# Layer 3 of a graph network as one stream: aligned node tiles summed in PSUM, PSUM operands for VectorE, nodes finished in the edge loop, experts by groups

## The chip, the core and the metric

The kernel runs on one core of a Trainium2 chip. Its engines are TensorE (PE), VectorE (DVE), ScalarE (ACT), GpSimd (POOL) and SyncE (SP); each works through its own queue of instructions in order, and semaphores make one wait for another. Layer 3's ordinary loads and stores are issued by SP, the indirect gathers and the accumulating writes by POOL. The metric is the device time of the whole program in microseconds (us); lower is better.

## The reference

Four layers, each a graph layer and a feed-forward layer, work on 3125 nodes of 256 float32 features. The graph has 50,000 edges, and one loop per node is added. The change is to layer 3, which is a graph attention (one row per edge, eight heads of 32) with a batch norm over the nodes, and then a mixture of four experts beside a shared network:

```python
e = jax.nn.leaky_relu(a_src[src] + a_dst[dst], NEG_SLOPE)
m = jax.ops.segment_max(e, dst, num_segments=N)
e = jnp.exp(e - m[dst])
denom = jax.ops.segment_sum(e, dst, num_segments=N)
alpha = e / denom[dst]
msg = xh[src] * alpha[:, :, None]
out = jax.ops.segment_sum(msg, dst, num_segments=N).reshape(N, H * D) + bias
out = (out - mean) * jax.lax.rsqrt(var + BN_EPS) * gamma + beta
...
gates = jax.nn.softmax(x @ gW + gb, axis=-1)
topv, topi = jax.lax.top_k(gates, TOPK)
topw = jax.nn.softmax(topv, axis=-1)
return shared + gated
```

The graph layer's input is the layer norm of x, and its result is added to x; the experts' input is again a layer norm of x, and their output is added to x too.

## The kernel before

Nodes lie in NT = 25 tiles of P = 128 rows. Edges are sorted by destination in an earlier layer and, with the loops, make ET = 416 tiles of 128, so that a tile's destinations lie close together. EL = 8 edge tiles are a chunk; there are NW = 52 chunks. Layers 0 to 2 come first and are nearly untouched. The end of layer 2 writes, for each node, a row of 264 numbers (projected features and a source term for each head) to DRAM as `xa_d`, and the destination terms, split into three bf16 parts, to `a_d` (`next_project`, lines 1003 to 1017). In layer 0's feed-forward part a table `acc3_d` of sums is filled with zeros (lines 1127 to 1130).

**The edge loop** is in `l3_gnn_sorted` (L547). The order of the work is that of the Python loop `for c in range(NW + LAG)` with LAG = 4: each engine takes its instructions in the order in which this loop makes them, and buffers of the pools (`bufs=`) set the waits. In iteration c:

- For chunk c, POOL gathers eight tiles of source rows from `xa_d` into the buffer `xa` (helper `gather`, L194), which has LAG + 3 = 7 copies. SP loads the destination numbers `dl`, from which DVE makes a bf16 one-hot `sT` (L384), and 128 rows of destination terms `aw` (L575): a window W0[c] that holds all destinations of the chunk. PE multiplies the two (`pa`, L582). DVE reduces the three parts (L585), adds the source terms once the gathers have landed (L589), and takes leaky ReLU and the maximum with the loop's own term (L590, L591: `top`).
- Every second iteration, `segment_max` takes two chunks at once: three transposes on PE (L405), two scans on DVE (L409, L410) and a maximum (L413). In the other iterations `segment_back` transposes it back, DVE subtracts (L604), ACT takes the exponential into the last columns of `xa` (L607), and DVE masks the loop's own term (L609).
- For chunk b = c - LAG, DVE multiplies features by exponentials in place (L616, 128 x 2048 elements, both operands in SBUF), makes a float32 one-hot of the destinations within the window (`onehot`, L390, comparing `iota` and `dloc`, both in SBUF), PE sums the edges of the window by eight products into `acc` (helper `mm`, L141), ACT copies it (L426), and POOL writes it to `acc3_d` by a DMA that adds (L427, `accumulate`). A window is not aligned with the node tiles, so a node's sum may be spread over several windows.

**After the loop**, DVE reads the sums back five tiles at a time (`fin`, L627), divides (L631 to L642), PE transposes each node tile (L646) and DVE takes its statistics (L647); `l3_norm` makes scale and shift, spreads them over the partitions, and DVE applies them and adds x tile by tile (L661 to L665). `l3_ffn` (L1784) then works through all nodes stage by stage: layer norm and transposes (L182, L189), logits (L1806), softmax (from L1702), the two largest of four (`first_max`), weights and their transposes (L1817 to L1828). Only then does it go by GROUPS of four node tiles (the seventh has one): shared layers and experts (L1836, L1852), the spread weights `pk` (L1857), the product `he` (L1859), the output product `po` and the addition to x (L1868), and the store.

Of the kernel before, what the change touches and what calls it, by code (L numbers as in the profile page):

```python
# [8 lines left out]
F32 = mybir.dt.float32  # L9
BF = mybir.dt.bfloat16  # L10
# [7 lines left out]
P = 128  # L18
# [8 lines left out]
EL = 8  # L27
# [8 lines left out]
W0 = [min(max(round(N * (g + 0.5) * EL * P / E) - P // 2, 0), NP - P) for g in range(NW)]  # L36

# [4 lines left out]
class Net:  # L42


    def __init__(self, ctx, tc, ins, out):
# [51 lines left out]
        self.acc3_d = self.dram.tile([NP, D + 16], F32, name="acc3_d")  # L97
# [216 lines left out]
    def prepare_flags(self):  # L314
# [4 lines left out]
        with ExitStack() as ctx:  # L319
# [28 lines left out]
            sums = work.tile([P, 3], F32, name="sums")  # L348
# [3 lines left out]
            out = work.tile([P, 2, ET], F32, name="out")  # L352
            nc.vector.tensor_scalar(out[:, 0], self.dloc, 0.0, None, op0=ALU.is_lt)
            nc.vector.tensor_scalar(out[:, 1], self.dloc, float(P - 1), None, op0=ALU.is_gt)
            nc.vector.tensor_reduce(sums[:, 1:3], out, axis=AX.X, op=ALU.add)
            nc.vector.tensor_reduce(sums[:, 0:1], sums, axis=AX.X, op=ALU.add)
# [38 lines left out]
    def segment_max(self, load, work, psum, al, s):  # L395
# [7 lines left out]
        aT = psum.tile([P, 3, P], F32, name="aT", bufs=1)  # L403
# [143 lines left out]
    def l3_gnn_sorted(self, wp):  # L547
        nc, tc = self.nc, self.tc
        bias = self.spread(wp, "L3_gnn_bias")
        gamma = self.plain(wp, "L3_gnn_gamma")  # L550
        beta = self.plain(wp, "L3_gnn_beta")
        R = D + 8
        with ExitStack() as ctx:
            xa_d, a_d, acc_d = self.xa_d, self.a_d, self.acc3_d
            big = ctx.enter_context(tc.tile_pool(name="big", bufs=1))
            xh = big.tile([P, NT, D], F32, name="xh")
            nc.sync.dma_start(xh, xa_d[:, :D].rearrange("(t p) d -> p t d", p=P))
            with ExitStack() as ctx1:
                big1 = ctx1.enter_context(tc.tile_pool(name="big1", bufs=1))
                load = ctx1.enter_context(tc.tile_pool(name="load", bufs=2))  # L560
                work = ctx1.enter_context(tc.tile_pool(name="work", bufs=3))
                psum = ctx1.enter_context(tc.tile_pool(name="psum", bufs=2, space=PSUM))

                top = big1.tile([P, ET + 2, 8], F32, name="top")
                nc.vector.memset(top[:, 0:1, :], -BIG)
                nc.vector.memset(top[:, ET + 1:, :], -BIG)
                LAG = 4
                xas, als = {}, {}
                mm = None
                for c in range(NW + LAG):  # L570
                    if c < NW:
                        t = c * EL
                        sT = self.window(load, c)
                        aw = load.tile([P, 48], BF, name="aw")
                        nc.sync.dma_start(aw, a_d[W0[c]:W0[c] + P, :, :]  # L575
                                          .rearrange("p i k -> p (i k)"))
                        xa = work.tile([P, EL, R + 8], F32, name="xa", bufs=LAG + 3)
                        xas[c] = xa
                        pa = psum.tile([P, EL, 3, 16], F32, name="pa")
                        for j in range(EL):  # L580
                            self.gather(xa[:, j, :R], xa_d, self.idx["src"][:, t + j:t + j + 1])
                            nc.tensor.matmul(pa[:, j].rearrange("p i k -> p (i k)"),  # L582
                                             sT[:, j * P:(j + 1) * P], aw, start=True, stop=True)
                        ao = work.tile([P, EL, 16], F32, name="ao", bufs=LAG + 1)
                        nc.vector.tensor_reduce(ao, pa.rearrange("p t i k -> p t k i"), axis=AX.X,  # L585
                                                op=ALU.add)
                        als[c] = ao
                        a = ao[:, :, :8]
# [1373 lines left out]
```

## Time and profile before

| what | value |
|---|---|
| runs, median of 3 | 4257.59 us (4254.7 to 4267.4) |
| the profiled execution: its own time | 4221.33 us |
| its span, first to last instruction | 4219.4 us |
| mean granted TensorE clock | 0.884 |
| busy: PE, DVE, ACT, POOL | 3351.4, 2125.7, 928.4, 1830.7 us |
| layer 3, first gather starts | 3171.94 us |
| last gather starts; DVE takes it up (L589) | 3846.98; 3851.34 us |
| last `acc` copied; last tile's statistics end | 3877.64; 3921.23 us |
| first scale and shift (L661) | 3925.1 us |
| expert groups begin to end in steps of | 30.5 us |

The page comes from one execution. A group names line, engine, operation, output and inputs, count, busy time, mean ns of one, and the idle time before it with what ended it. The slices cut the span into 40 parts of 105.5 us; a digit is the busy share in tenths, and PEclk is the clock that TensorE was granted, in tenths of full. The chunks repeat in pairs, because the segment maximum takes two.

### The profile page before, as it was taken

How to read it: one execution, taken by the hardware profiler on the slowest of the kernel's cores; microseconds unless marked ns; L12 is line 12 of the kernel's file. 1: busy time of each engine (PE TensorE's matmuls, PEld its weight loads, DVE VectorE, ACT ScalarE, POOL GpSimd, SP SyncE). 2: the span in 40 equal slices, each digit the busy share in tenths (PEclk: the TensorE clock that was granted, in tenths of full speed). 3: DMA queues.
4: the chain of work that ended last, by engine and by line, in shares of the span. 5: the costliest groups of instructions: out<-in, count | busy, mean ns of one | idle time of the engine just before them, and what ended most of it. 6: DMA issues, size and time to landing. Idle time of an engine off the chain costs nothing. (4 is left out here: it accounts for less than half of the span.)

```text
span 4219.4 us, 45504 instructions
## 1 busy us (share of the span) xinstructions
PE 3351.4 (79%) x15090; PEld 2224.8 (53%) x15090; DVE 2125.7 (50%) x5044; ACT 928.4 (22%) x1995; POOL 1830.7 (43%) x1561
## 2 busy tenths in 40 slices
PE   3598899999982649999999989999993434345599
PEld 2364377777761526666666645665562223223344
DVE  4672499999994354333333332233233444446610
ACT  2222200000001224333333323333330000000122
POOL 4200166666652037777777730000007888884000
PEclk7799999999996859999999999999995676777589
DMA  4641488888861867777777750000005555554000
GB/s 127 208 142 51 159 286 279 271 282 270 277 194 53 245 186 148 122 122 121 122 121 122 118 128 2 6 6 6 6 12 163 121 121 123 122 123 98 15 15 17
DMA packets 364151, 539.24 MB, mean 128 GB/s; under 512 B 75453, under 2 KB 271107, under 8 KB 363907
## 3 DMA queue, kind: packets, MB, share of 16 engines
q0 software_dynamic: 132528, 244.16, 27.8%
q1 hardware_dynamic: 223987, 284.74, 21.4%
q10 hardware_dynamic: 7392, 7.34, 0.5%
q8 instruction: 123, 2.02, 0.2%
q14 instruction: 121, 0.99, 0.1%
HBM read 393.40 MB, written 142.67 MB: 127 GB/s over the span
## 5 line engine op out<-in xcount | busy, mean ns | idle before, releaser
L194 POOL DMA_INDIRECT xa<-xa_d,src_i x416 | 504.1, 1212 | 819.7 <-DMA dl<-dlT_d 693.6
L794 POOL DMA_INDIRECT t<-sm,to x416 | 662.4, 1592 | 259.6 <-ACT sm L791 171.2
L194 POOL DMA_INDIRECT kv<-kv_d,src_i x416 | 418.4, 1006 | 604.0 <-DVE s L390 348.9
L141 PE MATMUL pf<-L_gnn_Wf,hf 128*128 128x256 f32 x1664 | 451.8, 394 | 0.0
L141 PE MATMUL pe<-L_gnn_We,ea 128*128 128x256 f32 x1664 | 437.5, 385 | 12.4 <-DMA ea<-in_edge_attr_dram 9.7
L780 DVE TENSOR_TENSOR xs<-xs,pf 128x512 f32<-128x512 f32 x208 | 142.8, 687 | 430.6 <-PE pf L141 429.0
L141 PEld LDWEIGHTS pe<-L_gnn_We,ea 128*128 128x128 f32 x1664 | 291.4, 192 | 67.2 <-DVE kv L504 26.9
L141 PEld LDWEIGHTS pf<-L_gnn_Wf,hf 128*128 128x128 f32 x1664 | 284.3, 191 | 50.0 <-ACT hf L742 0.5
L141 PEld LDWEIGHTS <-sT 128*128 128x128 bf16 x2496 | 240.4, 98 | 113.9 <-issue 22.8
L405 PE MATMUL aT<-ident,top 128*128 128x128 f32 x78 | 25.7, 395 | 339.3 <-DVE top L591 339.2
L141 PE MATMUL acc<-xa,s 128*128 128x272 f32 x832 | 258.3, 466 | 30.0 <-ACT acc_o L426 16.1
L504 DVE TENSOR_TENSOR kv<-kv,pe 128x1024 f32<-128x1024 f32 x208 | 250.2, 1203 | 4.9 <-PE pe L141 4.9
L426 ACT COPY acc_o<-acc 128x264 f32<-128x264 f32 (+1 forms) x104 | 39.7, 382 | 916.3 <-PE acc L141 485.7
L789 PE MATMUL ps<-xs,m 128*128 128x256 f32 x832 | 235.2, 405 | 1.6 <-DVE xs L780 0.8
L791 ACT COPY sm<-ps 128x512 f32<-128x512 f32 x208 | 121.7, 585 | 509.8 <-PE ps L789 428.7
L531 PE MATMUL acc<-kv,s 128*128 128x264 f32 x832 | 225.0, 395 | 11.1 <-DVE kv L526 8.9
L952 ACT ACTIVATE h<-ph,L_ffn_b,bn_r 128x512 f32<-128x512 f32 (+1 forms) x224 | 162.6, 731 | 290.7 <-PE ph L141 290.2
L141 PEld LDWEIGHTS acc<-xa,s 128*128 128x128 f32 x832 | 183.5, 231 | 79.3 <-ACT acc_o L426 24.6
L980 DVE SCALAR_TENSOR_TENSOR xres<-po,v,xres 128x256 f32<-128x256 f32 x200 | 96.1, 482 | 248.0 <-PE po L141 247.8
L589 DVE TENSOR_TENSOR ao<-ao,xa 128x64 f32<-128x64 f32 x52 | 11.7, 225 | 398.0 <-DMA xa<-xa_d,src_i 395.0
L405 PEld LDWEIGHTS aT<-ident,top 128*128 128x128 f32 x78 | 13.1, 181 | 357.8 <-DVE top L591 349.9
L141 PE MATMUL po<-L_ffn_Wo,h 128*128 128x256 f32 x800 | 196.2, 389 | 0.0
(400 smaller groups left out, 5868.7 us busy)
## 6 DMA issues: line engine op xcount, KB each, us to landing
ea<-in_edge_attr_dram SPq DMA_DIRECT2D x52, 1024.0 KB
dl<-dlT_d SPq DMA_DIRECT2D x156, 256.0 KB
row<-src_d SPq DMA_DIRECT2D x52, 512.0 KB
xs_d<-zero SPq DMA_DIRECT2D x2, 7168.0 KB
xg<-xs_d SPq DMA_DIRECT2D x28, 512.0 KB
t<-zero SPq DMA_DIRECT2D x4, 3328.0 KB
seg<-seg_d SPq DMA_DIRECT2D x52, 256.0 KB
qw<-q_d SPq DMA_DIRECT2D x52, 192.0 KB
```

The costliest lines, as they stand in the source:

```text
L141: self.nc.tensor.matmul(out, l, r, start=(i == 0), stop=(i == len(pairs) - 1))
L194: self.nc.gpsimd.indirect_dma_start(out=out, out_offset=None, in_=table, in_offset=bass.IndirectOffsetOnAxis(ap=ids, axis=0))
L405: nc.tensor.transpose(aT[:, i, :], al[:, 16 * s + i:16 * s + i + 16, :] .rearrange("p t h -> p (t h)"), self.ident)
L426: nc.scalar.copy(o, acc)
L504: nc.vector.tensor_add(kvv, kvv, pe[:, :, None, :].to_broadcast([P, 2, 2, D]))
L531: nc.tensor.matmul(acc, s1[:, j, :], kv[:, j, D:], start=((t + j) % EL == 0), stop=((t + j) % EL == EL - 1))
L780: nc.vector.tensor_mul(xs, xs, pf)
L789: nc.tensor.matmul(ps[:, j, :], m[:, (2 * c + j) % EL, :], xs[:, j, :], start=True, stop=True)
L791: nc.scalar.copy(sm, ps)
L794: nc.gpsimd.indirect_dma_start(out=tables[(2 * c + j) % len(tables)], in_=sm[:, j, :], in_offset=None, compute_op=ALU.add, out_offset=bass ...
L952: nc.scalar.activation(h[:, f, :w], ph[:, :w], AF.Relu, scale=ab[i][0][:, c:c + 1], bias=ab[i][1][:, c:c + 1])
L980: nc.vector.scalar_tensor_tensor(xv[:, i, :], po[:, i, :], v[:, j + i, e - 2:e - 1], xv[:, i, :], op0=ALU.mult, op1=ALU.add)
```

## The change

`l3_sorted` takes the place of `l3_gnn_sorted`, and `l3_dense` that of `l3_ffn` on this path.

- **Aligned tiles.** A table ENDS says which one or two node tiles an edge tile can touch (SPREAD = 38 nodes to either side of where it would lie if edges were spread evenly; layer 0 gets two more checks that the data keep to it, else the other, unsorted path runs). Each edge tile is multiplied once for each node tile that it can touch: 656 products of a one-hot and `xa` instead of 416, and as many `pa` products. W is the largest number of one-hots in a chunk, 16. A node tile's sum stays in PSUM (`acc`, bufs=3) from its first to its last edge tile: there is no `acc3_d`, no copy, no accumulating DMA and no reload. The bf16 destination terms stay in SBUF (`a3`).
- **PSUM operands.** `iota` is copied once to PSUM, and the exponential is written a second time, to the PSUM tile `back`; the multiply and the one-hots read those.
- **Buffers.** `xa` has LAG + 2 = 6 copies.
- **Nodes in the loop.** When a node tile's last edge tile is summed, the next iteration divides it (`finish`), and the one after transposes it and, every fourth tile, takes statistics (`stats`). Its own rows come by one load per tile.
- **Weights.** The feed-forward weights are loaded in iteration 4 (`l3_weights`); the biases `gb` and `sb3` are split in three bf16 parts (`bias3`), and their products are bf16.
- **Groups.** `l3_dense` does everything by groups of four node tiles: scale, shift and layer norm (`front`), transposes and logits (`turn`), softmax and choice (`choose`), weights' transposes (`spread`), and `experts`. The steps of the next group and the group after stand at three points (hooks) within the experts of a group.

The core of the diff (the loop's unchanged lines are left out, and the checks of layer 0 and the move of the code of layer 2 into a method of its own):

```diff
+PACE = N * P / E
+SPREAD = 38.0
+ENDS = [range(int(max(PACE * (t + 0.5) - SPREAD - 0.1, 0)) // P,
+              int(min(PACE * (t + 0.5) + SPREAD + 0.1, NP - 1)) // P + 1) for t in range(ET)]
-        self.acc3_d = self.dram.tile([NP, D + 16], F32, name="acc3_d")
...
-                        nc.sync.dma_start(aw, a_d[W0[c]:W0[c] + P, :, :]
-                                          .rearrange("p i k -> p (i k)"))
-                        xa = work.tile([P, EL, R + 8], F32, name="xa", bufs=LAG + 3)
...
-                        v = xa[:, :, :D].rearrange("p t (h c) -> p t h c", h=8)
-                        nc.vector.tensor_mul(v, v, xa[:, :, D:R].unsqueeze(3)
-                                             .to_broadcast([P, EL, 8, 32]))
-                        s1 = self.onehot(work, b * EL, EL)
-                        acc = psum.tile([P, R + 8], F32, name="acc")
-                        self.mm(acc, [(s1[:, j, :], xa[:, j, :]) for j in range(EL)])
-                        self.accumulate(work, acc_d, acc, b)
...
+            turn = psum.tile([P, 4, P], F32, name="turn")
+            iota = turn[:, 3, :]
+            nc.vector.tensor_copy(iota, self.iota)
...
+            def finish(T):
+                nonlocal oT
+                acc = accs.pop(T)
+                w = work.tile([P, 2, 8], F32, name="fw")
+                nc.vector.tensor_copy(w.rearrange("p i h -> p (i h)"), acc[:, D:D + 16])
+                den, z = w[:, 0, :], w[:, 1, :]
+                f = work.tile([P, 8], F32, name="fz")
+                nc.vector.tensor_add(den, den, z)
+                nc.vector.tensor_scalar(f, den, 0.0, None, op0=ALU.is_equal)
+                nc.vector.tensor_tensor(w, w, f[:, None, :].to_broadcast([P, 2, 8]), op=ALU.add)
+                nc.vector.reciprocal(den, den)
+                nc.vector.tensor_mul(z, z, den)
+                o = work.tile([P, 8, 32], F32, name="fo", bufs=2)
+                nc.vector.tensor_tensor(o, acc[:, :D].rearrange("p (h c) -> p h c", h=8),
+                                        den.unsqueeze(2).to_broadcast([P, 8, 32]), op=ALU.mult)
+                x4 = xh[:, T, :].rearrange("p (h c) -> p h c", h=8)
+                nc.vector.tensor_tensor(x4, x4, z.unsqueeze(2).to_broadcast([P, 8, 32]),
+                                        op=ALU.mult)
+                nc.vector.tensor_add(x4, x4, o)
+            def stats(T):
+                nonlocal oT
+                g, j = T // 4, T % 4
+                if j == 0:
+                    oT = work.tile([P, 2, 4 * P], F32, name="oT", bufs=1)
+                tp = psum.tile([P, 2, P], F32, name="tp")
+                for f in range(2):
+                    nc.tensor.transpose(tp[:, f, :], xh[:, T, f * P:(f + 1) * P], self.ident)
+                for f in range(2):
+                    nc.scalar.activation(oT[:, f, j * P:(j + 1) * P], tp[:, f, :], AF.Identity,
+                                         bias=bias[:, f:f + 1])
+                if j == 3 or T == NT - 1:
+                    w = min((T + 1) * P, N) - 4 * g * P
+                    for f in range(2):
+                        nc.vector.bn_stats(st[:, f, g, :], oT[:, f, :w])
+            for c in range(NW + LAG + 2):
+                for T in ready2:
+                    stats(T)
+                ready2 = []
+                for T in ready:
+                    finish(T)
+                    ready2.append(T)
+                ready = []
+                if c == 4:
+                    self.l3w = self.l3_weights(wp)
...
+                    xa = work.tile([P, EL, R + 8], F32, name="xa", bufs=LAG + 2)
...
+                    sT = load.tile([P, W, P], BF, name="sT")
+                    for T, js, k in parts[c]:
+                        nc.vector.tensor_scalar(sT[:, k:k + len(js), :], row[:, js[0]:js[-1] + 1, :],
+                                                float(W0[c] - T * P), self.part, op0=ALU.add,
+                                                op1=ALU.is_equal)
+                    for T, js, _ in parts[c]:
+                        if T not in seen:
+                            seen.add(T)
+                            nc.sync.dma_start(xh[:, T, :], self.xa_d[T * P:(T + 1) * P, :D])
+                    pa = psum.tile([P, EL, 3, 16], F32, name="pa")
+                    for j in range(EL):
+                        self.mm(pa[:, j].rearrange("p i k -> p (i k)"),
+                                [(sT[:, k + j - js[0], :], self.a3[:, T, :])
+                                 for T, js, k in parts[c] if j in js])
...
+                    back = psum.tile([P, 2, EL, 8], F32, name="back", bufs=2)
+                    nc.tensor.transpose(back.rearrange("p i t h -> p (i t h)"), mm, self.ident)
...
+                        nc.scalar.activation(m, aov[:, :, 0, :], AF.Exp)
...
+                b = c - LAG
+                if 0 <= b < NW:
+                    xa, ex = xas.pop(b), backs.pop(b)
+                    v = xa[:, :, :D].rearrange("p t (h c) -> p t h c", h=8)
+                    nc.vector.tensor_mul(v, v, ex.unsqueeze(3).to_broadcast([P, EL, 8, 32]))
+                    s1 = work.tile([P, W, P], F32, name="s", bufs=2)
+                    for T, js, k in parts[b]:
+                        n = len(js)
+                        t = b * EL + js[0]
+                        nc.vector.scalar_tensor_tensor(
+                            s1[:, k:k + n, :], iota[:, None, :].to_broadcast([P, n, P]),
+                            float(T * P),
+                            self.idxf["dst"][:, t:t + n].unsqueeze(2).to_broadcast([P, n, P]),
+                            op0=ALU.add, op1=ALU.is_equal)
+                    for T, js, k in parts[b]:
+                        begins = T not in accs
+                        if begins:
+                            accs[T] = psum.tile([P, 4 * P], F32, name="acc", bufs=3)
+                        for i, j in enumerate(js):
+                            nc.tensor.matmul(accs[T][:, :R + 8], s1[:, k + i, :], xa[:, j, :],
+                                             start=begins and i == 0,
+                                             stop=last[T] == b and j == js[-1])
+                        if last[T] == b:
+                            ready.append(T)
...
+            def front(g):
+                t0, n = GROUPS[g]
+                xv, ov = self.x[:, t0:t0 + n, :], o[:, t0:t0 + n, :]
+                nc.vector.tensor_mul(ov, ov, ab[:, None, 0, :].to_broadcast([P, n, D]))
+                nc.vector.tensor_add(xv, xv, ab[:, None, 1, :].to_broadcast([P, n, D]))
+                nc.vector.tensor_add(xv, xv, ov)
+                y = work.tile([P, 4, D], F32, name="y")
+                self.normalised(work, y, t0, n)
+                ys[g] = y
+            def turn(g):
+                t0, n = GROUPS[g]
+                y = ys.pop(g)
+                xT = xTs[g] = work.tile([P, 2, 4 * P], F32, name="xT")
+                for j in range(n):
+                    self.transposed(psum, xT, y[:, j, :], j)
+                pl = psum.tile([P, 4, NE], F32, name="sm", bufs=1)
+                for j in range(n):
+                    self.mm(pl[:, j, :], [(xT[:, k, j * P:(j + 1) * P], w_["gW"][:, k, :])
+                                          for k in range(2)] + [(self.ones3, w_["gb"])])
+                ws[g] = pl
...
+                hooks.get(0, lambda: None)()
...
+                    self.mm(po, [(hs[:, c], w_["sW3"][:, 0, :]), (self.ones3, w_["sb3"]),
+                                 (wT[:, j, :], w_["eb3"])]
+                            + [(he[:, i, c], w_["eW3"][:, i, :]) for i in range(2)])
+                    nc.vector.tensor_add(y[:, j, :], self.x[:, t, :], po)
...
+            front(0)
+            turn(0)
+            choose(0)
+            spread(0)
+            front(1)
+            for g in range(NG):
+                hooks = {}
+                if g + 1 < NG:
+                    def early(g=g):
+                        turn(g + 1)
+                        choose(g + 1)
+                    hooks[0] = early
+                    hooks[2] = lambda g=g: spread(g + 1)
+                if g + 2 < NG:
+                    hooks[1] = lambda g=g: front(g + 2)
+                experts(g, hooks)
```

## Prediction

> **What bounds the kernel now.** I read the slices of the span, the groups and the waits first, then the timeline of one steady pair of layer 3's edge chunks, then the tail by windows. The edge loop runs from 3172 to 3851 us (slices 31 to 37 of 40), where POOL leads; behind it come 368 us without POOL, in whose first half the tensor clock is low.
>
> ```profile
> span 4219.4 us, 45504 instructions
> POOL 4200166666652037777777730000007888884000
> PEclk7799999999996859999999999999995676777589
> L194 POOL DMA_INDIRECT xa<-xa_d,src_i x416 | 504.1, 1212 | 819.7 <-DMA dl<-dlT_d 693.6
> ```
>
> The 416 gathers take 1212 ns in the mean, but 948 in the median, so some are delayed. The waits between 3170 and 3880 us show that POOL never stands for a buffer (0.3 us of issue before each gather is all), and that DVE waits for what POOL brings:
>
> ```profile
> POOL xa L194 <- issue: 122.2, 402, 0.3
> DVE ao L589 <- DMA xa<-xa_d,src_i: 395.0, 51, 13.5
> ```
>
> From the timeline of the pair between 3502.69 and 3529.55 us (26.86 us; columns start, us, engine, line):
>
> ```profile
> 3506.83 1.95 POOL L194 DMA_INDIRECT xa<-xa_d,src_i  x1 [0.30 <-DVE seg_m L410]
> ...
> 3510.66 2.28 DVE L616 TENSOR_TENSOR xa<-xa 128x2048 f32<-128x2048 f32 x1
> 3510.89 2.86 POOL L194 DMA_INDIRECT xa<-xa_d,src_i  x1 [0.30 <-issue]
> ...
> 3514.06 0.94 POOL L194 DMA_INDIRECT xa<-xa_d,src_i  x1 [0.30 <-issue]
> ...
> 3517.49 1.03 POOL L427 DMA_DIRECT2D acc_d<-acc_o  x1
> ```
>
> The gather at 3510.89 ends 0.81 us after the message multiply L616 (3512.94); one that meets no such DVE operation takes 0.94. A pair is 16 gathers x 1.248 (0.948 + 0.30) = 20.0, two accumulates of 1.0, and 4.9 of delays: 26.9. The loop is POOL's. Layer 1 has the counter-example in its timeline: L504, with one operand in PSUM, runs from 1005.11 to 1006.31, and the gather at 1004.98 beside it takes 0.96.
>
> The tail's windows (PE, weight loads, DVE, ACT, POOL, clock, DMA share, GB/s): DVE alone, then PE at a low clock, then PE at full clock.
>
> ```profile
> 3925.00:3956.00 31.00, 0.72 (x4) 0.67 (x4) 30.88 (x105) 0.66 (x3) 1.17 (x4) 0.50 0.08 23
> 3956.00:4060.00 104.00, 101.61 (x319) 61.21 (x318) 23.05 (x102) 30.39 (x98) 0.00 (x0) 0.66 0.04 10
> 4060.00:4219.00 159.00, 152.29 (x436) 67.05 (x435) 17.12 (x35) 29.41 (x47) 0.00 (x0) 0.99 0.06 20
> ```
>
> [...] L504 with PSUM and L390 without both take 1.20 for 1024 elements[...] at 3503.64 the acc products come 8 in 3.84 us (0.48 each), at 3862 64 in 15.24 (0.238).
>
> **Edge loop, part by part.** From POOL's queue go the two accumulates, 2.0 us a pair. With the iota and a copy of exp in PSUM, multiply and one-hots no longer have two SBUF inputs: of the 4.9 I keep 0.3, for the small operations. These alone would leave 20.3 to 20.8 a pair. But a wait comes in. The xa buffers go from LAG+3 = 7 to LAG+2 = 6, so chunk c's first gather waits for the last acc product of chunk c-6. Those products (call them M) are issued in iteration c-2, where their one-hots stand in DVE's queue behind the add that waits for all eight gathers of chunk c-2. For an even chunk, DVE then does the add 0.22, the reduce of pa 0.54, leaky and top 0.44, a finished tile's operations (25 tiles over 26 pairs, 0.8 falling here), waits 0.4 for the third transpose, does two scans 1.33 and the first one-hot 1.0: 4.7. A pair's period, from its first gather to the next pair's:
>
> - to the start of its eighth gather 7 x 1.248 = 8.74;
> - landing 3.05 (the gather at 3499.64 starts DVE at 3502.69), delay left 0.3;
> - DVE 4.7;
> - M: alignment makes 416 tile products 656, that is 12.6 a chunk of two PE instructions each, 25.2. PE was idle, so 8 x 0.48 + 17.2 x 0.238 = 7.9; release 0.15.
>
> Sum 24.9, say 25.0. The odd chunk's wait is covered: its predecessor's gathers (10 us) outlast its M. The first six chunks find free buffers, 48 x 1.27 = 61 us; then 23 pairs x 25.0 = 575. The last gather lands some 636 us after the first starts; before 3851.34 - 3171.94 = 679.4. **Gain 43.** Bounds: M warm and a short DVE chain, 22.5 a pair, gain 101; PE at half clock throughout, M 12.1 and with a longer chain 28.6 a pair, loss 39. The clock in the loop before was 0.71 (3233 to 3851), between the two; I take the middle since PE will again idle ahead of M.
>
> The rest of the loop I cost at nothing, +-2 us: pa's extra bf16 products (240 x 0.035) and the statistics' transposes run while PE waits for gathers; the second exp on ACT (0.3 a chunk) is one iteration ahead of its reader; node rows come by 25 loads on SP and the 52 aw loads leave it, a queue that nobody waits for here; the expert weights at chunk 4 put a memset, selects and an iota of about 1.2 us on POOL. Outside the loop, DVE's extra checks in layer 0 (3 us) and the 3.4 MB of zeros no longer written (SP, near 230 us) stand beside work that nobody waits for; uncovered, the checks would cost 3. The order of each engine ahead of layer 3 is otherwise the same.
>
> **Tail, from landing.** Before: the remaining M, fin reloads and all tiles' sums and statistics to 3921.23, the affine from 3925.1 (+74), layernorm, transposes from 3956 (+105). After, 24 of 25 tiles are done in the loop: chain 4.7, five M of 6.0 (25.2 x 0.238) = 30, cold start 3.8, last tile 4.5, batchnorm's small operations 5: affine at +48 to +50; then only group 0's affine (three of 1.1) and layernorm (some 10): transposes from +64, 41 earlier. From there, before took 263.4: transposes and logits at the low clock, a softmax over all tiles (DVE waits 61.2 us for its logits), then groups of 30.5. After, a group on PE is 40 instructions x 0.477 = 19.1, output products 4 x 2.3 = 9.2 (2.85 before; sb3 becomes one bf16 product instead of 0.6), transposes and logits 4.2: 32.5, and 2 of waiting, as the multiplies he stand behind the next group's choice and the front of the one after in DVE's queue. Six groups x 34.5 = 207, start 5, last tile and its output 14: end at +290 against +368. **Gain 78.** Bounds: 60 (37.5 a group) and 90 (32.5).
>
> **Sum.** 43 + 78 = 121: a span of about 4098 for 4219.4. The profiled execution took 4221.33, 36 under the runs' median of 4257.59; I carry that difference over: 4257.59 - 121 = **4137**.
>
> **Rivals.**
> - A, 0.60: as above, the gathers paced by the buffer. Own range 4100 to 4180.
> - B, 0.17: the buffer hardly binds; a pair 22.5: 101 + 78, **4079**. For it: more PE work may keep M warm. Freely running gathers (20.8) would give 61 + 478, gain 218, 4040; against that, the chain is above 21 even with each term at its low end.
> - C, 0.14: PE stays at half clock in the loop; a pair 28.6: -39 + 78, **4219**. For it: the clock of 0.56 from 3171 to 3233. Against: 3.9 us of acc products were enough to be full, and M is longer now.
> - D, 0.04, slower: the expert groups serialise, PE waiting in each for DVE's choice and front and for the exps that stand among ACT's relus. It eats the gain from 34.5 + 121/6.25 = 54 us a group; at 60 it gives **4296**. Against: DVE has about 18 us of work a group, ACT 9.
> - E, 0.05: the PSUM operands don't free the gathers, so that the change doesn't do what it says, and the buffer's wait comes on top: a pair 29.5 (-60), tail +60: **4258**.
>
> **Numbers.** A measurement of this kernel tells 0.3%, 13 us, from no change. Faster: A, B, C and 0.02 of E, 0.93; within: 0.02 of E; slower: D and the rest of E, 0.05. The range 4060 to 4225 leaves out D, E, a quarter of B and of C, 0.17.
>
> **What would show it.** No gather over 1.4 us. First gathers of even chunks that wait 4 to 5 us for an acc product, odd ones that don't; a pair of 25. Affine at +50 after landing, groups of 34.5 at full clock. It is wrong if gathers still meet 2 us delays, if all of M comes at 0.48 an instruction, if the even chunks don't wait, or if PE waits over 10 us in a group.

## The result, and the profile after

The changed kernel took 4214.96 us (median of 4 runs, 4199.7 to 4223.2) against 4256.49 of the kernel before: a ratio over the runs of 0.9893, 95% interval 0.9857 to 0.9929 (the two medians alone give 0.990). It is faster by 41.5 us, about 1%. The forecast was 121 us, 4137; the range of 4060 to 4225 holds the time, the likeliest case's own range (4100 to 4180) doesn't.

The profiled execution took 4221.72 us. Its page, the lines that answer to those of before:

```profile
span 4220.0 us, 47001 instructions
...
POOL 4200246666651226777777760000004445554200
PEclk8799999999996758999999998999996677777889
...
L198 POOL DMA_INDIRECT xa<-xa_d,src_i x416 | 395.6, 951 | 348.5 <-PE back L690 184.1
```

The gathers are as short as forecast (951 ns in the mean, the longest 1.19 us), but the 8s of the loop have become 4s and 5s: POOL stands still. Three stretches compared with the profile before: layer 3's first gather starts at 3210.8 instead of 3171.9 (+38.9); from there to the last landing's add it takes 745.1 instead of 679.4 (**+65.7**, forecast -43); from there to the end 264.1 instead of 368.1 (**-104.0**, forecast -78). The two spans are equal within a microsecond, and yet the runs differ by 41; the experiments below give a reading of that.

Waits in the loop, 3210 to 3950 us (engine, tile and line, what was waited for, us, times, longest):

```profile
POOL xa L198 <- PE back L690: 184.1, 16, 28.0
...
DVE ao L680 <- DMA xa<-xa_d,src_i: 124.9, 27, 6.2
...
DVE seg_m L422 <- remote: 57.8, 9, 8.1
DVE ao L676 <- remote: 43.9, 7, 11.8
```

The first line is the forecast wait for a buffer, named after the PE instruction next to the last `acc` product. The last two were not forecast. They are the scan on the third `turn` transpose and the sum of `pa`, both waiting for PE, and "remote" says that the profile sees nothing on this core that ends the wait. One pair of the timeline shows why:

```profile
3495.56 0.48 PE L418 MATMUL turn<-ident,top 128*128 128x128 f32 x1
...
3501.38 0.95 POOL L198 DMA_INDIRECT xa<-xa_d,src_i  x1 [0.30 <-issue]
3501.68 0.69 DVE L422 TENSOR_TENSOR_SCAN seg_m<-seg,turn 128x256 f32<-128x256 f32 x1 [5.44 <-issue]
...
3504.50 8.34 PE L726 MATMUL acc<-xa,s 128*128 128x272 f32 x28 [1.05 <-issue]
...
3513.11 0.94 POOL L198 DMA_INDIRECT xa<-xa_d,src_i  x1 [10.79 <-PE back L690]
```

The transpose ends at 3496.04, and the scan that needs it starts 5.6 us later. Until the scan has run, DVE can't make the one-hots and PE can't multiply, so POOL's next gather waits 10.8 us instead of 4 to 5. Call a start late by the time from when both its input was made and DVE was free. Eleven of the 26 first scans then start 68 us late in sum, and nine of the 52 sums of `pa` 79. In the profile before none was late. From the ninth chunk on, the pairs of the loop (first gather to the next pair's) fall into two groups: seven of 23.4 to 25.3 us, near the forecast 25.0, and the others of 26.6 to 34.3; the mean is 29.0.

The tail (windows; columns as in the prediction): the first from the last landing to the first affine, the second to PE's next work, the third to the end.

```profile
3956.00:4003.00 47.00, 37.17 (x159) 29.59 (x157) 32.54 (x82) 6.48 (x19) 0.00 (x0) 0.93 0.00 1
4003.00:4020.00 17.00, 3.79 (x19) 3.28 (x18) 16.45 (x38) 2.96 (x8) 0.00 (x0) 0.50 0.00 0
4020.00:4220.00 200.00, 194.48 (x689) 101.85 (x688) 66.71 (x293) 63.83 (x119) 0.00 (x0) 0.91 0.05 17
```

The affine stands at +47 (forecast 48 to 50), the transposes at +60 (forecast 64; they begin 4 us before the second window ends), and PE is busy for 194 of the last 200 us. Between 4122.90 and 4151.50 one group takes 28.6 us of unbroken PE work; from the end of the first group to that of the sixth it is 29.5 a group, where 34.5 was forecast.

### The profile page after: what moved, and what is told of

It is laid out like the page before. It is cut to its first block, busy times and chain, and to the rows that moved or that the text cites. A ratio compares the mean times of both kernels' runs of the same rounds, so it can differ in the third digit from the quotient of the medians.

```text
span 4220.0 us, 47001 instructions
## 1 busy us (share of the span) xinstructions
PE 3424.5 (81%) x15760; PEld 2321.6 (55%) x15760; DVE 2205.8 (52%) x5396; ACT 943.8 (22%) x2024; POOL 1669.0 (40%) x1510
## 5 line engine op out<-in xcount | busy, mean ns | idle before, releaser
L198 POOL DMA_INDIRECT xa<-xa_d,src_i x416 | 395.6, 951 | 348.5 <-PE back L690 184.1
L726 PE MATMUL acc<-xa,s 128*128 128x272 f32 x1312 | 365.1, 443 | 96.0 <-issue 94.6
L145 PEld LDWEIGHTS <-sT 128*128 128x128 bf16 x3152 | 273.0, 101 | 277.7 <-issue 185.1
L726 PEld LDWEIGHTS acc<-xa,s 128*128 128x128 f32 x1312 | 281.8, 219 | 169.6 <-issue 101.1
L517 DVE TENSOR_TENSOR kv<-kv,pe 128x1024 f32<-128x1024 f32 x208 | 250.9, 1206 | 24.5 <-remote 20.0
L145 PE MATMUL qx<-qw,sT 128*128 128x256 bf16 x1248 | 190.6, 275 | 5.6 <-issue 3.0
L145 PE MATMUL ph<-xT,L_ffn_W 128*128 128x512 f32 (+1 forms) x448 | 185.5, 553 | 0.5 <-ACT h L1213 0.5
L145 PE MATMUL ph<-h,L_ffn_W 128*128 128x512 f32 (+1 forms) x448 | 183.0, 549 | 0.0
```

What stands on the lines that cost most here:

```text
L145: self.nc.tensor.matmul(out, l, r, start=(i == 0), stop=(i == len(pairs) - 1))
L198: self.nc.gpsimd.indirect_dma_start(out=out, out_offset=None, in_=table, in_offset=bass.IndirectOffsetOnAxis(ap=ids, axis=0))
L517: nc.vector.tensor_add(kvv, kvv, pe[:, :, None, :].to_broadcast([P, 2, 2, D]))
L726: nc.tensor.matmul(accs[T][:, :R + 8], s1[:, k + i, :], xa[:, j, :], start=begins and i == 0, stop=last[T] == b and j == js[-1])
```

## The experiments

After the first comparison the theory was this: the loop is paced by the buffer as forecast, and late signals from PE come on top. Open was what makes them late: the new order of the loop, the operands, the uninterrupted gathers, or the execution. The table has all the runs but the two probes, in the order of the text; "chip" is the number of the chip that a run was made on ("?" where it isn't known), "loop" is from the first gather to the last landing's add, "tail" from there to the end, both from the run's profile; the mean pair is taken from the ninth chunk to the 51st; "marks" is how many of the 16 landing marks that each gather leaves are found in the trace of the loop's middle.

| kernel | chip | loop, mean pair | tail | marks | ratio to before, interval |
|---|---|---|---|---|---|
| before, first profile | ? | 679.4, 26.6 | 368.1 | 16 | |
| changed, first profile | ? | 745.1, 29.0 | 264.1 | 3 | 0.9893 (0.9857 to 0.9929) |
| changed again | 8 | 755.9, 29.6 | 265.9 | 3 | 0.9924 (0.9907 to 0.9942) |
| before again | 8 | 683.5, 26.6 | 367.9 | 15 | 1.0001 (0.9984 to 1.0019) |
| changed, operands in SBUF | 8 | 648.1, 24.7 | 254.7 | 7 | 0.9627 (0.9574 to 0.9680) |
| before, operands in PSUM | 8 | 622.1, 23.7 | 367.2 | 3 | 0.9816 (0.9766 to 0.9867) |
| changed, only iota in PSUM | 8 | 752.0, 29.1 | 266.7 | 9 | 0.9904 (0.9872 to 0.9936) |
| changed, POOL pauses | 8 | 780.3, 30.6 | 266.3 | 7 | 0.9977 (0.9963 to 0.9991) |
| before, PSUM and new tail | 8 | 625.0, 23.9 | 293.5 | 3 | 0.9671 (0.9629 to 0.9713) |
| changed, seven buffers | 6 | 561.4, 21.6 | 255.9 | 16 | 0.9446 (0.9399 to 0.9493) |
| before, PSUM, six buffers | 6 | 655.2, 26.0 | 361.1 | 16 | 0.9947 (0.9927 to 0.9967) |
| changed, a third time | 9 | 648.8, 25.2 | 266.3 | 16 | 0.9675 (0.9643 to 0.9706) |
| changed, seven buffers | 9 | 558.6, 21.5 | 255.8 | 16 | 0.9441 (0.9413 to 0.9470) |
| changed, operands in SBUF | 9 | 631.1, 24.5 | 254.7 | 16 | 0.9623 (0.9593 to 0.9653) |
| before, operands in PSUM | 9 | 576.8, 22.3 | 363.6 | 16 | 0.9738 (0.9709 to 0.9768) |

### Both kernels again

> The changed kernel unaltered, profiled a second time. In its first profile the edge loop (first gather to last landing) took 745 us instead of the forecast 636, and in nine pairs DVE started the scan on the third transpose 1.5 to 8 us after that transpose had ended, while PE stood still behind it. Theory A, the order of the new loop makes this (PE's next product waits for DVE while DVE waits for PE): again 741 +-15 us in the loop, some ten scans late, though not in the same pairs, time 4215 +-10. Theory B, it was a state of that one execution: no late scans, pairs of 25.0, the loop at 636 to 660 and the profiled execution near 4120 to 4140.

> The kernel before unaltered, profiled a second time; its first profile was 36 us under the median of its runs and showed no late scan. Theory A (late starts belong to the new loop): loop 679 +-5 us, no scan late by over 1 us; the 36 us, if they come, lie ahead of layer 3, which then starts near 3208 instead of 3172. Theory B (a state of an execution): some scans are late here too, and the 36 us lie partly in the loop.

The changed kernel repeats its loop (756 us, twelve scans more than 1.2 us late), so it was no accident of one execution; its time, 4232, lies 7 over the range of theory A. The kernel before has its loop at 683.5, with no late scan but a few other late starts, and layer 3 begins at 3193 instead of 3172. Theory A's numbers came in for the loop, its cause isn't shown by that; and that layers 0 to 2 lose time too, with the same instructions, doesn't fit a cause in the new loop.

### The operands, taken away and added alone

```diff
 changed kernel:
-            iota = turn[:, 3, :]
-            nc.vector.tensor_copy(iota, self.iota)
+            iota = self.iota
...
-                        nc.scalar.activation(m, aov[:, :, 0, :], AF.Exp)
...
-                    xa, ex = xas.pop(b), backs.pop(b)
+                    xa = xas.pop(b)
+                    ex = xa[:, :, D:R]
 kernel before:
+                iota = psum.tile([P, P], F32, name="iotap", bufs=1)
+                nc.vector.tensor_copy(iota, self.iota)
...
+                            nc.scalar.activation(m, aov[:, :, 0, :], AF.Exp)
...
-                        nc.vector.tensor_mul(v, v, xa[:, :, D:R].unsqueeze(3)
+                        nc.vector.tensor_mul(v, v, ex.unsqueeze(3)
...
```

> The changed kernel with the message multiply's exp and the one-hots' iota read from SBUF as before (the copies in PSUM and the second exp are left out). If the PSUM operands are what freed the gathers: gathers of 2 to 3 us return, their mean goes from 951 to about 1200 ns, which is 4 us a pair; where the pair is paced by the buffer only the delays of the last gathers before the wait count, so +50 to +110 us, time 4265 to 4325. Rival, the loop is paced by the chain from landing through DVE and PE and the delays fall into its waits: within 15 us of the changed kernel.

> The kernel before with only the PSUM operands added (iota and a copy of exp in PSUM), seven buffers, aligned windows and accumulates as they were. Theory: POOL alone paces the loop, so a pair falls from 26.86 to 20.3 to 20.8 plus two accumulates of 1.0, 22.3 to 22.8; 26 pairs save 106 to 118 us: 4140 to 4152. Rival, the freed gathers run into the buffer's wait here too, or DVE becomes the bound: a pair of 24.5 to 26, 20 to 60 us saved: 4197 to 4237.

Both expectations for the first one failed: without the PSUM operands the changed kernel isn't slower but 130 us faster (4102.5 against 4232.3 on the same chip). The gathers are delayed again (mean 1186 ns, up to 3.2 us), the pair is 24.7, and POOL hardly waits for a buffer (17.9 us in the loop, 17.6 of it at once). In the kernel before, the same operands gain, but 622 us is more than the 585 to 600 that POOL's sum of 22.3 a pair gives; its sums of `pa` wait 172 us for "remote". So the PSUM operands free POOL (no gather takes over 1.17 us in the kernel before with them), and on this chip free gathers go with late signals.

### Is it the free gathers?

The probe puts a ping-pong ahead of the loop (PE transposes, DVE copies back, each waiting for the other) with 32 gathers a stretch beside it:

```diff
+                    self.gather(slots[:, j, :], self.xa_d, self.idx["src"][:, j:j + 1])
...
+                nc.tensor.transpose(pp, ball, self.ident)
+                nc.vector.tensor_copy(ball, pp)
```

> The changed kernel with five stretches put ahead of layer 3's loop, so that its output stays and its time grows by some 250 us. In each stretch PE transposes a 128x128 tile, DVE copies it back, and so on 48 times: each waits for the other. Stretch 0: no gathers. 1: POOL issues 32 row gathers back to back beside it. 2: the same, with a POOL memset of 512 columns (0.5 us) after every fourth gather. 3: as 1, with a DVE add of two SBUF operands (1024 columns) after every fourth copy. 4: as 3, but one operand of the add in PSUM. Read: from a transpose's end to the start of its copy. Theory P (gathers issued without a pause hold back PE's completions): under 0.3 us in 0, stalls of 3 to 30 us in 1 and 4, few and short ones in 3, where the add stops POOL; 2 tells whether a memset is pause enough. Theory Q (DVE's operands in PSUM hold PE up): stalls in 4 alone. Theory R (PE standing behind a wait is enough): stalls in all five, or in none if it needs the loop's order.

Nothing tied the adds to the ping-pong, so they ran first and the stretches mixed; only what ran beside what can be read. With no gather beside them, from 3379 us on, 144 rounds took 0.86 us each. Beside free gathers most were on time too (0.86, and 1.33 with an add between), but from 3296 to 3329 twelve took 2.80 (timeline):

```profile
3298.20 0.29 DVE L586 COPY ball<-pp 128x128 f32<-128x128 f32 x1 [2.51 <-remote]
3298.54 0.95 POOL L198 DMA_INDIRECT slots<-xa_d,src_i  x1 [0.30 <-issue]
...
3298.55 0.47 PE L585 MATMUL pp<-ident,ball 128*128 128x128 f32 x1 [2.33 <-issue]
...
3301.00 0.29 DVE L586 COPY ball<-pp 128x128 f32<-128x128 f32 x1 [2.51 <-remote]
```

PE answers DVE's copy within 0.06 us (3298.49 to 3298.55), but DVE hears of PE's end at 3299.02 only at 3301.00. No operand lies in PSUM here but the transpose itself, and no loop order is involved. The gathers of that stretch ended at 3323; from 3329 on the round fell by steps, 2.10, 1.41, 0.86. Earlier it went the other way too: DVE's copy ends at 3258.95, and PE takes its result up at 3263.52.

```profile
3258.68 0.27 DVE L586 COPY ball<-pp 128x128 f32<-128x128 f32 x1
...
3263.52 0.47 PE L585 MATMUL pp<-ident,ball 128*128 128x128 f32 x1 [5.83 <-remote]
```

So it is the signals that are late, not PE's work that is slow. Of theory P this leaves that rounds were late only beside gathers or just behind them; Q falls.

```diff
 changed kernel, only iota in PSUM:
-                        nc.scalar.activation(m, aov[:, :, 0, :], AF.Exp)
...
+                    ex = xa[:, :, D:R]
 changed kernel, POOL pauses:
                         self.gather(xa[:, j, :R], self.xa_d, self.idx["src"][:, t + j:t + j + 1])
+                        if j % 4 == 3:
+                            for _ in range(5):
+                                nc.gpsimd.memset(rest, 0.0)
```

> The changed kernel with the exp of the message multiply read from SBUF again (second exp left out) and only the iota of the one-hots in PSUM. Each multiply again stops POOL once a chunk for up to 2.3 us, the one-hots don't. Theory P (PE's completions are held back while POOL gathers without a pause): these stops let them through, late starts on DVE fall from 160 to 200 us in the loop to under 80, the loop is at most 660 us, time 4090 to 4130. Theory Q (DVE reading PSUM is the cause, the one-hots being one half of it): late starts of 80 to 150 us, the loop 690 to 730, time 4150 to 4200.

> The changed kernel with five small POOL memsets (0.2 us each and their gaps, some 1.2 us) after every fourth gather, both PSUM operands kept. Theory P with any stop of the gathers being enough: late starts fall under 60 us, a pair is 16 x 1.248 + 4 x 1.2 = 24.8 by POOL or 25 by the buffer, the loop 630 to 660, time 4095 to 4140 although 125 us of POOL work are added. Theory Q, or a POOL that must stand still altogether: the late starts stay, loop 740 to 790, time 4210 to 4260.

Both speak against theory P in its simple form. Stops of 2 us at each multiply (64 gathers that meet one take 1.92 in the mean, the others 0.96) leave the loop at 752, and memsets on POOL make it longer (780). The late starts of scans and sums of `pa` did fall, to 78 and 87 us from 147, and yet the loop didn't get shorter; these late starts alone don't account for it. Why the place of the one-hots' `iota` makes 100 us on chip 8 (752 against 648) stays unexplained.

```diff
-        run(net.l1_gnn_sorted, net.after_l1_gnn_sorted, net.l3_gnn_sorted, net.l3_ffn)
+        run(net.l1_gnn_sorted, net.after_l1_gnn_sorted, net.l3_gnn_sorted)
...
-            self.l3_norm(big, psum, st, gamma, beta, xh, None)
+            a, b = self.batchnorm(big, st, gamma, beta)
+            self.l3_dense(wp, xh, a, b)
```

> The kernel before with the two PSUM operands and the changed kernel's tail (expert weights loaded behind the loop, gate and experts by groups of four tiles); edge loop, accumulates in memory and the separate pass over the node tiles as before. The groups alone account for the gain behind the affine: affine at +74 as before, from there 217 us as in the changed kernel (264 less 47) plus the weight loads (up to 10): tail 291 to 301 instead of 367, so 66 to 76 us under the kernel with the PSUM operands alone, 4112 to 4125. If the groups need the early finish of the tiles to pay, tail 330 to 360.

As expected: the tail is 293.5 with the groups alone, 74 less than with the old expert code. The changed kernel's 264 to 266 leave some 28 us to nodes finished in the loop.

### The buffer, and the probe with a fixed order

```diff
 changed kernel, seven buffers:
-                if c == 4:
-                    self.l3w = self.l3_weights(wp)
...
-                    xa = work.tile([P, EL, R + 8], F32, name="xa", bufs=LAG + 2)
+                    xa = work.tile([P, EL, R + 8], F32, name="xa", bufs=LAG + 3)
...
-        w_ = self.l3w
...
+            w_ = self.l3_weights(ctx.enter_context(tc.tile_pool(name="wd", bufs=1)))
 kernel before with PSUM operands, six buffers:
-                        xa = work.tile([P, EL, R + 8], F32, name="xa", bufs=LAG + 3)
+                        xa = work.tile([P, EL, R + 8], F32, name="xa", bufs=LAG + 2)
 second probe:
+                    nc.vector.scalar_tensor_tensor(wide2, wide, ball[:, 0:1], add, op0=ALU.mult,
+                                                   op1=ALU.add)
```

> The changed kernel with seven gather buffers instead of six, both PSUM operands kept; to make room the expert weights are loaded at the head of the tail instead of in the fourth chunk. Theory B (signals of PE that reach the other engines late are what lengthens the loop, and with six buffers POOL stands still for each of them): the first gathers of even chunks no longer wait, the late starts on DVE stay (100 to 200 us in sum), the loop falls from 745 to 600 to 640 us, the tail grows by up to 15 (weights): 4070 to 4125. Rival C (DVE or PE itself is the bound of the new loop): a pair of 28 to 30 as before, loop 720 or more, time 4200 to 4235.

> The kernel before with the two PSUM operands, and six gather buffers instead of seven: the reverse of the run with seven buffers. Its chain from landing to the last acc product is only 19 to 20 us (16 instructions of 0.24 instead of 25 of 0.3), so that on time signals would hide the wait for the buffer entirely. Theory B: late signals of 5 to 20 us now stop POOL: the loop grows from 622 to 680 to 750 us, time 4245 to 4315. Rival D (only the 25 products of an aligned chunk make the buffer bind): loop 620 to 640, time 4185 to 4205.

> As the first probe, with the order of the stretches fixed, 48 gathers a stretch, and the adds tied to the ping-pong: 60 rounds without gathers; 60 beside gathers; 40 beside gathers with an add of two SBUF operands (1024 columns) after every second round; 40 beside gathers with one operand of the add in PSUM; 40 with that add and no gathers; 60 beside gathers; 60 without. A round on time takes 0.86 us, one with an add about 2.1 every second time. Theory P2 (gathers that nothing interrupts slow the signals): on time in stretches 1, 5 and 7, rounds of 1.4 to 6 us in 2, 4 and 6 from 10 to 25 us after the first gather on, and hardly any in 3. Rival Q2 (the PSUM operand matters by itself): late rounds in 5 as well, fewer in 2 and 6 than in 4.

All three profiles show something new: every landing mark is in the trace, layer 3 starts at 3169 and 3171 in the two without a probe, and DVE takes up PE's results on time (the sums of `pa` wait 1.0 us for their products in the whole loop with seven buffers and 1.9 with six, and none for "remote"). The second probe's rounds beside free gathers and without an add (57 and 58 in its two stretches) all took 0.86 us (timeline; the gathers and the copies of one stretch):

```profile
3226.13 0.95 POOL L198 DMA_INDIRECT slots<-xa_d,src_i  x1 [0.30 <-issue]
3226.14 0.18 PEld L580 LDWEIGHTS pp<-ident,ball 128*128 128x128 f32 x1 [0.68 <-DVE ball L581]
3226.14 0.48 PE L580 MATMUL pp<-ident,ball 128*128 128x128 f32 x1 [0.39 <-DVE ball L581]
3226.65 0.29 DVE L581 COPY ball<-pp 128x128 f32<-128x128 f32 x1 [0.57 <-PE pp L580]
```

Theory P2 and its rival both fall: free gathers alone are not enough. These three runs were made on another chip. So theory B, which took late signals for granted, isn't tested by the two runs with the buffers changed. The loop of the unaltered changed kernel, which stands behind the probe in that run, took 641 us with pairs of 25.2. Seven buffers brought far more than expected (561 us). With six buffers in the kernel before, the pairs alternate between 28 and 23.3, and of the even chunks every second waits 7 to 8 us at its first gather, although nothing is late: the sixth buffer binds by itself, which neither theory had expected.

### The same kernels on a third chip

> The changed kernel unaltered, a third time, beside the kernel before on the same chip. The late signals were in every profile taken on one chip (number 8 of the jobs) and in none taken on another (number 6): there the very loop of the changed kernel, run behind the second probe, took 641 us with pairs of 25.2. Theory E (late signals are a property of the chip that runs it): where the trace shows every landing's record and no late start, the loop takes 635 to 645 and the time is 4065 to 4090, a ratio to the kernel before of 0.960 to 0.968; where it shows thinned records, the loop takes 740 to 760 and the ratio is 0.988 to 0.994. Rival F (it was the probe ahead of the loop that put it in order): late starts and 740 to 760 us on either kind.

> The changed kernel with seven gather buffers again. On a chip with signals on time as before: ratio 0.940 to 0.950. On one with late signals, theory B: the seventh buffer hides most of them, the loop 600 to 660 us instead of 750, ratio 0.953 to 0.968. Rival: late signals cost the same with seven buffers, loop 700 or more, ratio over 0.975.

> The changed kernel with both operands back in SBUF, again. It is paced by POOL (24.66 a pair: 16 x 1.248 and 4.7 of delays) and never waited for a buffer. On a chip with signals on time it should then be within 15 us of the changed kernel itself, whose pair is 25.2: the PSUM operands alone bring nothing, since the buffer's wait takes what they free; ratio 0.960 to 0.968. On one with late signals 0.958 to 0.968, that is 110 to 130 us faster than the changed kernel, as the first time.

> The kernel before with the two PSUM operands alone, again. On a chip with signals on time a pair is 22.3 (POOL), the loop 585 to 600 us, ratio 0.978 to 0.983; on one with late signals 622 us and 0.977 to 0.987 as the first time.

Theory E's numbers come in, with the loop 4 us and the time 1 us over their upper ends, and rival F falls, as no probe ran ahead: on chip 9, whose traces hold all marks, the unaltered changed kernel took 4091.2 us against 4223.5, **132 us faster**. The same waits and the same pair of its loop, 3178 to 3820 us:

```profile
POOL xa L198 <- PE back L690: 90.0, 14, 12.0
...
DVE seg_m L422 <- PE turn L418: 2.7, 11, 0.4
```

```profile
3495.74 0.48 PE L418 MATMUL turn<-ident,top 128*128 128x128 f32 x1 [6.04 <-DVE top L682]
...
3496.58 0.68 DVE L422 TENSOR_TENSOR_SCAN seg_m<-seg,turn 128x256 f32<-128x256 f32 x1
```

The "remote" lines are gone, and the scan starts 0.36 us after its transpose, behind another DVE instruction. With both operands in SBUF it is 27 us faster still (4064.4; at most 15 apart was expected): POOL then never waits for a buffer (below, nearly all of its waits are the 0.3 us before each gather), and a pair of 24.5 set by delayed gathers (up to 4.2 us) is no worse than one of 25.2 set by the buffer. Between the two profiles lie 38 us: 9 ahead of layer 3, 18 in the loop and 12 in the tail. The tail gains since PE lags less: 119 `acc` instructions are left to it after the last landing instead of 143, and the affine stands at +37.1 instead of +47.5.

```profile
POOL xa L198 <- issue: 112.4, 363, 1.8
```

Seven buffers let the free gathers pay (that run also loads the weights behind the loop; what this alone does was not run). The page of that kernel on chip 9, 3989.6 us, ratio 0.9441, the quickest of all:

```profile
span 3989.1 us, 47013 instructions
...
POOL 4200066666662204777777776000000176776200
```

The kernel before with the PSUM operands alone has pairs of 22.3, POOL's own sum, and not one late wait. Its loop of 577 us and its ratio of 0.9738 beat the expected 585 to 600 and 0.978 to 0.983.

## Why the prediction was wrong, and where it was right

**The steps that failed.** Between the two first profiles two terms of the sum missed. The edge loop, "Gain 43", lost 65.7 us, with a pair of 29.0 for 25.0; and the stretch ahead of it, "Outside the loop", put at nothing or 3 us of checks, grew by 38.9. What the forecast had put at 0.15 us or at nothing is the time from the end of an engine's work to the moment when another engine hears of it: in the loop 68 us at scans and 79 at sums of `pa`, where the profile before had none. The one hint of it on hand was the 36 us between that profile and the runs, and **the last step of the sum, which failed with these two**, took them for a constant: "The profiled execution took 4221.33, 36 under the runs' median of 4257.59; I carry that difference over".

The 36 us are no constant. On chips 6 and 9 the kernel before takes 4227.5 and 4223.5, near its profile; on chip 8 it takes 4255 to 4259, as in the first runs. So the profile looks like one from a chip with signals on time, and the runs, like those of the changed kernel, like chip 8's; their chips aren't known.

Between the two kinds of chip lie 25 us for the kernel before (the span of its second profile less that of its first: 21 ahead of layer 3, 4 in the loop; by the medians 28 to 36), and 127 for the changed one (4220.0 less 4093.4: 32.5 ahead of layer 3, 96.3 in the loop, -2.2 in the tail). The 96 are all in one wait: from the seventh chunk on, the first gathers of even chunks wait 226 us in sum in the first profile and 130 on chip 9. The clock isn't what differs: the mean granted clock of the kernel before is 0.88 on all three chips. The first comparison contains the difference of the 127 and the 25.

**Made on one kind of chip, the sum holds.** The changed kernel's profile on chip 9 less the first profile before: -126.0 us, forecast -121. That it is so near is in part luck: the loop gained 12 less than forecast, the tail 24 more, and layer 3 started 6.4 later. By terms:

- *Edge loop*, forecast 636 and gain 43: 648.8, gain 30.6. The pair, forecast 25.0, is 25.19, the even chunks' waits are 5.7 in the mean (130 us in 23, forecast 4 to 5), the odd ones have none, no gather takes over 1.54. What is missing are the first six chunks, 73.0 instead of 61; what delays them wasn't pursued. On chip 8 and in the first profile this same term measures 29.0 to 29.6 a pair and 88 for the first six chunks.
- *Tail*, forecast gain 78: 101.8, and 104.0 in the first profile. Mis-sized was the group, 34.5: in the stretch of 28.6 us shown above, the busy times of its kinds of product add up to 33.2 (32.5 in the forecast), but the kinds overlap, so that PE is busy for 28.6, and the 2 us of waiting aren't there. Five steps of 29.5 instead of 34.5 are 25 of the 26 us.
- *PSUM operands*: they free the gathers, as forecast (with SBUF operands on chip 9, gathers that meet a multiply take 2.09 us in the mean, those that meet a one-hot 1.25, others 0.96; with PSUM operands 0.95 or 0.96 in all three cases); what in the chip makes this so was not shown. But with six buffers they gain nothing in the changed kernel, whose pair was then the buffer's; the forecast credited them without asking what the loop would be with neither.
- *The M part* of the chain, 7.9 for 25.2 instructions: 8.3 for 28 in the pair shown, 7.5 for 24 in a pair on chip 9 (from 3475.24), so 7.5 and 7.9 for 25.2. Its two speeds are those of the profile before, where PE stands for 15.1 us (to 3503.37), then takes 3.84 for 8 products (from 3503.64), and soon after 3.37 for 14 (from 3508.73). The release, put at 0.15 by estimate, is 0.27 in the pair shown and 0.28 on chip 9. The clock of the loop is 0.71 in the first profile and 0.74 on chip 9 (0.69 before), while PE's busy time in it is 383 and 385 us (264 before): 119 us more of PE's work went with a clock only 0.02 higher in the first profile.

Rival B (a pair of 22.5, the buffer hardly binding) came only with a seventh buffer. C's numbers, 28.6 a pair and 4219 us, are nearly those of the runs, but not its mechanism: late signals lengthened the pair, and on chip 9, with M as long, it is 25.2. That the range holds 4214.96 is luck too. D fell, since PE doesn't stand in the groups (busy for all 28.6 us of the one above), and E, since the gathers are free (951 ns). No rival had a wait whose signal is late.

## What to carry to other kernels

Before a profile is set against a median, ask whether both come from the same conditions: a difference between them that one kernel hides may be multiplied by the next one, and here a chain without slack paid for each late signal. A change that frees an engine and takes away its buffer in one stroke should be costed in both orders; on chip 9 freeing POOL was worth -27 us with six buffers, and by estimate 75 with seven (4064.4, with the operands in SBUF and six buffers, less 3989.6; seven with SBUF operands were not run, but POOL waits for no buffer there already with six). Where a changed kernel stands still, look at whether the wait's end matches the end of the instruction waited for, before a cause is sought in the order.

## What the runs showed of the hardware that was not expected

Signals between engines came late by far more than the work took: up to 29 us from the end of PE's `pa` products to DVE's start in the first profile. On chip 8 this went with gathers issued back to back and with landing marks missing from the trace (about 3 of 16 left in the changed loop, 15 in the loop before); on chips 6 and 9 the same gathers left all marks and no late start. In the slow stretch of the probe the late rounds stand 0.7 us apart (1.41, 2.10, 2.80; on time it is 0.86). The ends of PE's work are modelled in the records, so that PE's side alone could be read as a slow PE; that PE, too, heard of DVE 4.6 us late speaks for the signals. That it is the chip is the plainest reading, not shown: chip 8 was used in two sittings, the first two, and chips 6 and 9 in one each after them, and no kernel went back to chip 8, so that something else which ended in between would look the same. Why it happens, and whether the recording of the trace takes part in it, stays open too. Seven buffers were not run on chip 8, so what they hide there isn't known.
